# A graph layer and a two-expert FFN in one kernel: smaller layer-norm pieces, whole-pair selections, one engine for the last factor

## The chip, the cores and the metric

The kernel runs on one core of a Trainium2 chip. A core has five engines that run their own instruction streams and meet at semaphores: PE (TensorE, matrix products), DVE (VectorE, element-wise work and statistics), ACT (ScalarE, functions of the form f(scale·x + bias)), POOL (GpSimd, programmable; here it also writes the descriptors of gathers) and SP (SyncE, here only a queue that issues DMAs). Data lies in the on-chip memory of 128 partitions (SBUF); PE writes its sums into a second, small memory (PSUM).

The metric is the device time of one execution in microseconds (us), the median of several runs; less is better.

## The reference

Only what matters here:

```python
def _layernorm(x, axis=-1, eps=1e-05):
    return (x - mean(x)) / sqrt(var(x) + eps)

# x: 12500 nodes x 256; 200000 edges (src, dst, edge_weight), sorted by dst
def gnn(X, src, dst, val, W, b):
    msgs = (X @ W)[src] * val[:, None]
    return segment_sum(msgs, dst, 12500) + b

def ffn(x):                      # x[1, 12500, 256], 8 experts, hidden 512
    # routing from the mean over all nodes: the two best experts, weights tw
    out = sum over the two experts of tw_e * (gelu(x W1_e + b1_e) W2_e + b2_e)
    return layer_norm(out + x) * gamma + beta

x = x + gnn(_layernorm(x))
x = x + ffn(_layernorm(x)[None])[0]
```

## The kernel before, in words

Everything is float32. The work has three stages.

**First layer norm (lines 359 to 381).** `groups` cuts the 12500 nodes into pieces of up to R·128 nodes. With R = 8 there are 12 pieces of 1024 nodes (1 MB each) and two small ones, 14 in all. For each piece SP issues the load of `xt` (L362), DVE takes the statistics of each of the eight rows per partition (`row_stats`, L58 and L59), adds eps (L65), POOL raises to the power −1/2 (L66), DVE makes −mean/std (`nm`, L369), ACT writes the normalised rows in place (L373, eight instructions) and issues the store to `xn` in the chip's main memory (L376). ACT then clears one fourteenth of `acc`, the array of sums (L378). The pool `ln` has four buffers. `load_segment(0)`, three loads of edge data on SP (L297), stands ahead of the loop; `prepare_segment(0)` (L299 to L353: small DVE work, two products on PE, one copy on ACT) stands after the third piece.

**The gather loop.** Edges are taken 128 at a time as a column; four columns make a step and two steps a pair (`GB`, `SUPER`), so a pair has eight gathers. For each pair POOL issues eight indirect DMAs (`gather_pair`, L432), each of which brings 128 rows of `xn` by the 128 source indices of a column. `select` has DVE make, for each column, a 128x32 matrix with the edge's weight at its destination's place (`sel`, L415, with `iota`, `rel` and `wgt`) and for each step a 128x128 matrix `spread` (L423). `multiply` first has PE do a small product into `all_in` (L448) that reads every gathered column, so that later ones need no waits of their own, and then the eight products `pt` (L453); ACT copies them (L456), `spread_out` multiplies by `spread` (L468) and DVE adds into `acc` (L487). Between pairs the order written by hand in the main loop (with budgets in microseconds, `PAIR_US` and others) puts other work: `product`, `normalised` and `transposed` finish a block of 256 nodes whose sums are complete, and `work` runs parts of the experts' products (L604, L612) whose results go to `yts`.

**The end.** When the last pair is added, the last block is finished, the routing is computed, and 25 iterations follow, one for each group of up to 512 nodes, in a pipeline four deep. In an iteration `q` PE mixes the two experts' results (`mixed`), then `store(q-3)` has DVE add the node's own value (L849) and SP issue the output, `put(q-2)` multiplies by gamma (L843, on POOL when its number is odd and on DVE when it is even), `normalise(q-1)` has DVE make `nmt` (L833) and ACT normalise (L835), and `measured(q)` has DVE take statistics (L58, L59), add eps (L823) and POOL take the power (L825). Each engine works in this program order.

Of the kernel before, what the change touches and what calls it, by code (L numbers as in the profile page):

```python
# [18 lines left out]
P = 128  # L19
# [9 lines left out]
GB = 2  # L29
# [1 line left out]

NB = 8

R = 8

TB = 256
TPB = TB // P
# [24 lines left out]
def inv_std(nc, pool, out, var, half, rows, n):  # L62

    ve = pool.tile([P, R], FP, name="ve")
    nc.vector.tensor_scalar(ve[:rows, :n], var, EPS, None, ALU.add)  # L65
    nc.gpsimd.tensor_tensor(out, ve[:rows, :n], half[:rows, :n], ALU.pow)  # L66
# [30 lines left out]
def gnn_ffn_kernel(  # L97
# [43 lines left out]
    nc.vector.memset(ones, 1.0)  # L141
    row = const.tile([1, P], FP, name="row")
    nc.vector.memset(row, 1.0)
    zero = const.tile([P, 1], FP, name="zero")
    nc.vector.memset(zero, 0.0)
# [12 lines left out]
    viol = const.tile([P, 1], FP, name="viol")  # L158
    cand_f = const.tile([1, SLOTS], FP, name="cand_f")
    iota_i = const.tile([P, P], I32, name="iota_i")  # L160
    nc.gpsimd.iota(iota_i, pattern=[[1, P]], base=0, channel_multiplier=0)
    iota = const.tile([P, P], FP, name="iota")
    nc.vector.tensor_copy(iota, iota_i)
# [90 lines left out]
    with tc.tile_pool(name="rt", bufs=1) as rt, tc.tile_pool(  # L254
# [19 lines left out]
        def scratch_ps():  # L274
# [8 lines left out]
        nc.tensor.matmul(  # L283
            bias_ps.rearrange("p k d -> p (k d)"), row, bias_row.rearrange("p k d -> p (k d)"), start=True, stop=True
        )
        edgep = open_pool(name="edges", bufs=2)
        segment = {}

# [3 lines left out]
        def load_segment(k):  # L292
            s0, n = segs[k]
            t = {}
            for name, ap, dt in (("src_i", src, I32), ("dst_i", dst, I32), ("wgt", edge_weight, FP)):
                t[name] = edgep.tile([P, SEG * SUPER], dt, name=name)
                nc.sync.dma_start(t[name][:, : n * SUPER], ap[:, s0 * SUPER : (s0 + n) * SUPER])  # L297
            segment[k] = t
# [59 lines left out]
        cleared, part_n = 0, -(-(H * (NT * P + WIN)) // len(groups(N)))  # L358
        with tc.tile_pool(name="ln", bufs=4) as lp, tc.tile_pool(name="ln_s", bufs=8) as ls:
            for g, (r0, n, rows) in enumerate(groups(N)):  # L360
                xt = lp.tile([P, R, D], FP, name="xt")
                nc.sync.dma_start(xt[:rows, :n], x[r0 : r0 + rows * n].rearrange("(p r) d -> p r d", r=n))  # L362
                mv = ls.tile([P, R, 2], FP, name="mv")
                rs = ls.tile([P, R], FP, name="rs")
                nm = ls.tile([P, R], FP, name="nm")
                for r in range(n):
                    row_stats(nc, ls, mv[:rows, r], rows, xt[:rows, r])
                inv_std(nc, ls, rs[:rows, :n], mv[:rows, :n, 1], half, rows, n)
                nc.vector.scalar_tensor_tensor(  # L369
                    nm[:rows, :n], mv[:rows, :n, 0], -1.0, rs[:rows, :n], op0=ALU.mult, op1=ALU.mult  # L370
                )
                for r in range(n):
                    nc.scalar.activation(  # L373
                        xt[:rows, r], xt[:rows, r], AF.Identity, bias=nm[:rows, r : r + 1], scale=rs[:rows, r : r + 1]
                    )
                nc.scalar.dma_start(xn[r0 : r0 + rows * n].rearrange("(p r) d -> p r d", r=n), xt[:rows, :n])  # L376
                m = min(part_n, H * (NT * P + WIN) - cleared)
                nc.scalar.activation(acc_f[:, cleared : cleared + m], zero.to_broadcast([P, m]), AF.Copy)  # L378
# [12 lines left out]
        all_in = psum("in_ps", 1).tile([P, GB * SUPER], FP, name="all_in")  # L391

        w1 = expp.tile([P, SLOTS, H, F], FP, name="w1")
        w2 = expp.tile([P, SLOTS, FC, D], FP, name="w2")
# [10 lines left out]
        def select(i):  # L405

            s0, n = pairs[i]
            sel = selp.tile([P, GB * SUPER, NARROW], FP, name="sel")
            spread = selp.tile([P, GB, WIN], FP, name="spread")
            for j in range(n):  # L410
                k, at = seg_of(s0 + j)
                t = segment[k]
                for c in range(SUPER):
                    col = slice(at * SUPER + c, at * SUPER + c + 1)
                    nc.vector.tensor_scalar(  # L415
                        sel[:, j * SUPER + c],
                        iota[:, :NARROW],
                        t["rel"][:, col],
                        t["wgt"][:, col],
                        ALU.is_equal,  # L420
                        ALU.mult,
                    )
# [417 lines left out]
        def put(q, v):  # L840
            bb, n = mixes[q]
            m, t0 = n * TPB, bb * 2 * TPB
            (nc.gpsimd if q % 2 else nc.vector).tensor_tensor(  # L843
                v[:, :m], v[:, :m], gam.unsqueeze(1).to_broadcast([P, m, D]), ALU.mult
            )
            return v, m, t0
# [267 lines left out]
```

## Time and profile before

| what | value |
|---|---|
| median of three runs | 2258.58 us (2256.89 to 2259.1) |
| the profiled execution: its own time, its span | 2254.92 us, 2253.1 us |
| granted TensorE clock, mean | 0.865 |
| busy: PE, PE weight loads, DVE | 1506.6, 1175.2, 1173.3 us |
| busy: ACT, POOL | 523.3, 1573.4 us |
| first gather starts; last gather starts | 107.3 us; 2063.6 us |
| busy in 0 to 107.3 us: DVE, ACT, POOL | 58.99, 74.84, 22.10 us |
| busy in 2140.9 to 2253.1 us: PE, DVE, POOL | 71.13, 93.23, 54.33 us |

Span is the time from the first to the last instruction that the profiler saw. The page lists groups of instructions by line, engine, operation and tile, written output<-input; "x1564" is their count, then come busy microseconds and the mean nanoseconds of one, then the idle time of the engine just before them and what ended it. "issue" means that the engine waited for nothing that the profile shows.

### The profile page before, as it was taken

How to read it: one execution, taken by the hardware profiler on the slowest of the kernel's cores; microseconds unless marked ns; L12 is line 12 of the kernel's file. 1: busy time of each engine (PE TensorE's matmuls, PEld its weight loads, DVE VectorE, ACT ScalarE, POOL GpSimd, SP SyncE). 2: the span in 40 equal slices, each digit the busy share in tenths (PEclk: the TensorE clock that was granted, in tenths of full speed). 3: DMA queues.
4: the chain of work that ended last, by engine and by line, in shares of the span. 5: the costliest groups of instructions: out<-in, count | busy, mean ns of one | idle time of the engine just before them, and what ended most of it. 6: DMA issues, size and time to landing. Idle time of an engine off the chain costs nothing. (4 is left out here: it accounts for less than half of the span.)

```text
span 2253.1 us, 29981 instructions
## 1 busy us (share of the span) xinstructions
PE 1506.6 (67%) x9662; PEld 1175.2 (52%) x9662; DVE 1173.3 (52%) x4519; ACT 523.3 (23%) x1114; POOL 1573.4 (70%) x1626
## 2 busy tenths in 40 slices
PE   0034544445488888888765564988888888886875
PEld 0023333333267666666553343766666667664775
DVE  5535565655465565555454444544534443433687
ACT  5701111111122222222111111222222222221332
POOL 1277777777777777777777777777777777774254
PEclk9977677666799999999787776999999999999897
DMA  6634444444455555555544445555555545454585
GB/s 230 252 110 123 138 134 124 137 124 124 132 183 158 170 158 165 159 163 152 147 133 141 124 129 155 153 161 151 161 152 161 152 148 153 152 153 135 194 277 199
DMA packets 157377, 353.15 MB, mean 157 GB/s; under 512 B 34764, under 2 KB 65822, under 8 KB 154142
## 3 DMA queue, kind: packets, MB, share of 16 engines
q0 software_dynamic: 75072, 205.10, 32.0%
q1 hardware_dynamic: 79478, 132.85, 17.4%
q10 hardware_dynamic: 2664, 13.20, 1.4%
q8 instruction: 81, 1.33, 0.2%
q14 instruction: 82, 0.67, 0.1%
HBM read 286.89 MB, written 64.14 MB: 156 GB/s over the span
## 5 line engine op out<-in xcount | busy, mean ns | idle before, releaser
L432 POOL DMA_INDIRECT g<-xn,src_i x1564 | 1481.1, 947 | 485.0 <-issue 457.3
L487 DVE TENSOR_TENSOR acc<-acc,ps 128x256 f32 x391 | 164.0, 419 | 545.4 <-PE ps L468 397.5
L448 PE MATMUL all_in<-g,sel 128*32 128x8 f32 (+1 forms) x392 | 43.5, 185 | 591.9 <-issue 347.6
L604 PE MATMUL ph<-zTj,w 128*128 128x256 f32 x1568 | 388.8, 391 | 8.8 <-DMA zTj<-zts 8.8
L612 PE MATMUL po<-hT,w 128*128 128x256 f32 x1568 | 381.8, 388 | 12.3 <-DVE yT L618 12.3
L415 DVE TENSOR_SCALAR sel<-iota,rel,wgt 128x32 f32<-128x32 f32 x1564 | 371.6, 323 | 7.3 <-DMA xn<-xt 7.3
L448 PEld LDWEIGHTS all_in<-g,sel 128*32 128x32 f32 x392 | 29.9, 117 | 653.5 <-issue 551.0
L612 PEld LDWEIGHTS po<-hT,w 128*128 128x128 f32 x1568 | 303.1, 196 | 56.6 <-DVE yT L618 15.1
L604 PEld LDWEIGHTS ph<-zTj,w 128*128 128x128 f32 x1568 | 302.1, 198 | 50.1 <-issue 6.3
L456 ACT ACTIVATE part<-pt 128x512 f32<-128x512 f32 (+1 forms) x196 | 116.7, 595 | 844.4 <-PE pt L453 844.4
L468 PEld LDWEIGHTS ps<-spread,part 128*128 128x128 f32 x1564 | 250.2, 244 | 109.4 <-issue 109.4
L605 ACT ACTIVATE hT<-ph,b 128x256 f32<-128x256 f32 x392 | 185.6, 473 | 514.7 <-PE ph L604 514.7
L468 PE MATMUL ps<-spread,part 128*128 128x128 f32 x1564 | 293.6, 345 | 1.1 <-DVE acc L487 1.1
L453 PE MATMUL pt<-g,sel 128*32 128x256 f32 x3128 | 272.6, 470 | 0.0
L618 DVE SCALAR_TENSOR_TENSOR yT<-po,b,zTj 128x256 f32<-128x256 f32 x196 | 85.7, 479 | 252.2 <-PE po L612 251.0
L453 PEld LDWEIGHTS pt<-g,sel 128*32 128x32 f32 x3128 | 106.4, 127 | 43.5 <-issue 23.8
L512 PE MATMUL gz<-wg,acc 128*128 128x256 f32 x392 | 105.5, 416 | 24.9 <-ACT zT L545 13.9
L423 DVE TENSOR_SCALAR spread<-iota,slot 128x128 f32<-128x128 f32 x391 | 121.0, 309 | 0.0
L825 POOL TENSOR_TENSOR rst<-vet,half 128x4 f32<-128x4 f32 (+1 forms) x25 | 42.4, 1697 | 107.1 <-DVE vet L823 107.1
L512 PEld LDWEIGHTS gz<-wg,acc 128*128 128x128 f32 x392 | 78.7, 207 | 43.6 <-ACT zT L545 19.3
L513 DVE TENSOR_TENSOR acc<-gz,xt 128x512 f32<-128x512 f32 x49 | 33.9, 691 | 127.6 <-PE gz L512 127.6
L527 ACT ACTIVATE z<-acc,nmz,rstds 128x256 f32<-128x256 f32 x98 | 53.2, 591 | 128.1 <-DVE acc L487 117.0
(153 smaller groups left out, 1151.2 us busy)
## 6 DMA issues: line engine op xcount, KB each, us to landing
zTj<-zts SPq DMA_DIRECT2D x98, 256.0 KB
yts<-yT SPq DMA_DIRECT2D x98, 256.0 KB
g<-xn,src_i POOLq DMA_INDIRECT x1564, 2.8
ab<-yts SPq DMA_DIRECT2D x48, 512.0 KB
zts<-zT SPq DMA_DIRECT2D x49, 256.0 KB
xt<-in_x SPq DMA_DIRECT2D x12, 1024.0 KB
xn<-xt ACTq DMA_DIRECT2D x12, 1024.0 KB
xt<-in_x SPq DMA_DIRECT2D x48, 256.0 KB
```

Source lines behind the costliest of these rows:

```text
L415: nc.vector.tensor_scalar(sel[:, j * SUPER + c], iota[:, :NARROW], t["rel"][:, col], t["wgt"][:, col], ALU.is_equal, ALU.mult,)
L423: nc.vector.tensor_scalar(spread[:, j], iota[:, :WIN], t["slot"][:, at : at + 1], None, ALU.is_equal)
L432: nc.gpsimd.indirect_dma_start(out=g[:, j], out_offset=None, in_=xn, in_offset=bass.IndirectOffsetOnAxis(ap=segment[k]["src_i"][:, col : c ...
L453: nc.tensor.matmul(pt[q, j // SUPER], sel[:, j], g[:, j], start=True, stop=True, tile_position=(0, j % SUPER * NARROW))
L456: nc.scalar.activation(part[:, :n], pt[:, :n], AF.Copy)
L468: nc.tensor.matmul(ps[:, j, h], part[:, j, h * P : (h + 1) * P], spread[:, j], start=True, stop=True)
L487: nc.vector.tensor_tensor(at, at, ps[:, j], ALU.add)
L512: nc.tensor.matmul(ps[:, j], node_tile(t0 + j)[:, h], wg[:, h], start=(h == 0), stop=(h == H - 1))
L604: nc.tensor.matmul(ph, w1[:, k, h, c * P : (c + 1) * P], zT[:, h], start=(h == 0), stop=(h == H - 1))
L605: nc.scalar.activation(hT[:, c], ph, AF.Gelu, bias=b1[:, k, c : c + 1])
L612: nc.tensor.matmul(po[:, h], w2[:, k, c, h * P : (h + 1) * P], hT[:, c], start=(c == 0), stop=(c == FC - 1))
L618: nc.vector.scalar_tensor_tensor(yT[:, i], po[:, i], b2[:, k, i : i + 1], zT[:, i], op0=ALU.add, op1=ALU.add)
```

## The change

Eight edits:

1. `R` is 4: the first layer norm has pieces of 512 nodes (512 KB), 24 of them and two small ones, 26 in all, in nine buffers.
2. Its loop is split into `measure(g)` and `write(g)`; `write(g-1)` comes after `measure(g)`. `load_segment(0)` comes after `measure(1)`, `prepare_segment(0)` after the fifth piece.
3. A part of `acc` (128x975) is cleared by a POOL memset after each piece, not by ACT.
4. `iota_i` and `bias_row` lie in pools that are closed after use, and the two loads of `bias_row` stand beside the product that reads them.
5. `select` makes all eight `sel` matrices of a pair in two DVE instructions on 128x256 elements (compare, then multiply by the weight in place) and both `spread` matrices in one.
6. The small product that reads every gathered column goes to the head of `pt`; the PSUM tile `all_in` is gone.
7. `put` is always on POOL.
8. `zero` is gone, as nothing reads it.

```diff
-R = 8
+R = 4
...
-    bias_row = const.tile([1, 2, D], FP, name="bias_row")
-    nc.scalar.dma_start(bias_row[:, 0], b_gnn[None, :])
-    nc.scalar.dma_start(bias_row[:, 1], beta[None, :])
...
+        with tc.tile_pool(name="once", bufs=1) as once:
+            bias_row = once.tile([1, 2, D], FP, name="bias_row")
+            nc.scalar.dma_start(bias_row[:, 0], b_gnn[None, :])
+            nc.scalar.dma_start(bias_row[:, 1], beta[None, :])
+            nc.tensor.matmul(
+                bias_ps.rearrange("p k d -> p (k d)"), row, bias_row.rearrange("p k d -> p (k d)"), start=True, stop=True
+            )
...
-        load_segment(0)
-        with tc.tile_pool(name="ln", bufs=4) as lp, tc.tile_pool(name="ln_s", bufs=8) as ls:
-            for g, (r0, n, rows) in enumerate(groups(N)):
+        parts = groups(N)
+        with tc.tile_pool(name="ln", bufs=9) as lp, tc.tile_pool(name="ln_s", bufs=4) as ls:
+
+            def measure(g):
+                r0, n, rows = parts[g]
                 xt = lp.tile([P, R, D], FP, name="xt")
                 nc.sync.dma_start(xt[:rows, :n], x[r0 : r0 + rows * n].rearrange("(p r) d -> p r d", r=n))
...
+            measured_last = None
+            for g in range(len(parts)):
+                new = measure(g)
+                if g == 1:
+                    load_segment(0)
+                if measured_last:
+                    write(*measured_last)
+                measured_last = new
                 m = min(part_n, H * (NT * P + WIN) - cleared)
-                nc.scalar.activation(acc_f[:, cleared : cleared + m], zero.to_broadcast([P, m]), AF.Copy)
+                nc.gpsimd.memset(acc_f[:, cleared : cleared + m], 0.0)
                 cleared += m
-                if g == 2:
+                if g == 4:
                     prepare_segment(0)
+            write(*measured_last)
...
-            for j in range(n):
-                k, at = seg_of(s0 + j)
-                t = segment[k]
-                for c in range(SUPER):
-                    col = slice(at * SUPER + c, at * SUPER + c + 1)
-                    nc.vector.tensor_scalar(
-                        sel[:, j * SUPER + c], iota[:, :NARROW], t["rel"][:, col], t["wgt"][:, col],
-                        ALU.is_equal, ALU.mult,
-                    )
-                nc.vector.tensor_scalar(spread[:, j], iota[:, :WIN], t["slot"][:, at : at + 1], None, ALU.is_equal)
+            k, at = seg_of(s0)
+            t, m = segment[k], n * SUPER
+            cols = slice(at * SUPER, at * SUPER + m)
+            shape = [P, m, NARROW]
+            nc.vector.tensor_tensor(
+                sel[:, :m], iota[:, :NARROW].unsqueeze(1).to_broadcast(shape),
+                t["rel"][:, cols].unsqueeze(2).to_broadcast(shape), ALU.is_equal,
+            )
+            nc.vector.tensor_tensor(
+                sel[:, :m], sel[:, :m], t["wgt"][:, cols].unsqueeze(2).to_broadcast(shape), ALU.mult
+            )
+            shape = [P, n, WIN]
+            nc.vector.tensor_tensor(
+                spread[:, :n], iota[:, :WIN].unsqueeze(1).to_broadcast(shape),
+                t["slot"][:, at : at + n].unsqueeze(2).to_broadcast(shape), ALU.is_equal,
+            )
...
-                all_in[:NARROW, : n * SUPER], sel[:, n * SUPER - 1], g[:, : n * SUPER, 0], start=True, stop=True
+                pt[:NARROW, 0, : n * SUPER], sel[:, n * SUPER - 1], g[:, : n * SUPER, 0], start=True, stop=True
...
-            (nc.gpsimd if q % 2 else nc.vector).tensor_tensor(
+            nc.gpsimd.tensor_tensor(
                 v[:, :m], v[:, :m], gam.unsqueeze(1).to_broadcast([P, m, D]), ALU.mult
             )
```

More of the change, by code (lines that the diff above doesn't have):

```diff
@@ L143, in gnn_ffn_kernel @@
     nc.vector.memset(row, 1.0)
-    zero = const.tile([P, 1], FP, name="zero")
-    nc.vector.memset(zero, 0.0)
     wg = const.tile([P, H, D], FP, name="wg")
@@ L159, in gnn_ffn_kernel @@
     cand_f = const.tile([1, SLOTS], FP, name="cand_f")
-    iota_i = const.tile([P, P], I32, name="iota_i")
-    nc.gpsimd.iota(iota_i, pattern=[[1, P]], base=0, channel_multiplier=0)
     iota = const.tile([P, P], FP, name="iota")
-    nc.vector.tensor_copy(iota, iota_i)
+    with tc.tile_pool(name="once", bufs=1) as once:
+        iota_i = once.tile([P, P], I32, name="iota_i")
+        nc.gpsimd.iota(iota_i, pattern=[[1, P]], base=0, channel_multiplier=0)
+        nc.vector.tensor_copy(iota, iota_i)
     place_i = const.tile([P, 1], I32, name="place_i")
@@ L282, in gnn_ffn_kernel @@
         bias_ps = biasp.tile([P, 2, D], FP, name="bias_ps")
-        nc.tensor.matmul(
-            bias_ps.rearrange("p k d -> p (k d)"), row, bias_row.rearrange("p k d -> p (k d)"), start=True, stop=True
-        )
+        with tc.tile_pool(name="once", bufs=1) as once:
+            bias_row = once.tile([1, 2, D], FP, name="bias_row")
[4 more added lines that the diff above has]
+            )
         edgep = open_pool(name="edges", bufs=2)
@@ L353, in prepare_segment @@
             t.update(base_i=base_i, rel=rel, slot=slot)
-        load_segment(0)
         acc_f = acc.rearrange("p h n -> p (h n)")
-        cleared, part_n = 0, -(-(H * (NT * P + WIN)) // len(groups(N)))
-        with tc.tile_pool(name="ln", bufs=4) as lp, tc.tile_pool(name="ln_s", bufs=8) as ls:
-            for g, (r0, n, rows) in enumerate(groups(N)):
+        parts = groups(N)
+        cleared, part_n = 0, -(-(H * (NT * P + WIN)) // len(parts))
+        with tc.tile_pool(name="ln", bufs=9) as lp, tc.tile_pool(name="ln_s", bufs=4) as ls:
+            def measure(g):
+                r0, n, rows = parts[g]
                 xt = lp.tile([P, R, D], FP, name="xt")
@@ L364, in gnn_ffn_kernel @@
                 rs = ls.tile([P, R], FP, name="rs")
-                nm = ls.tile([P, R], FP, name="nm")
                 for r in range(n):
@@ L368, in gnn_ffn_kernel, with write @@
                 inv_std(nc, ls, rs[:rows, :n], mv[:rows, :n, 1], half, rows, n)
+                return g, xt, mv, rs
+            def write(g, xt, mv, rs):
+                r0, n, rows = parts[g]
+                nm = ls.tile([P, R], FP, name="nm")
                 nc.vector.scalar_tensor_tensor(
@@ L390, in gnn_ffn_kernel @@
         pps, aps = psum("part_ps", 1), psum("agg_ps", 1)
-        all_in = psum("in_ps", 1).tile([P, GB * SUPER], FP, name="all_in")
         w1 = expp.tile([P, SLOTS, H, F], FP, name="w1")
@@ L409, in select @@
             spread = selp.tile([P, GB, WIN], FP, name="spread")
-            for j in range(n):
-                k, at = seg_of(s0 + j)
-                t = segment[k]
-                for c in range(SUPER):
-                    col = slice(at * SUPER + c, at * SUPER + c + 1)
[L415 to L422, printed above, removed]
-                nc.vector.tensor_scalar(spread[:, j], iota[:, :WIN], t["slot"][:, at : at + 1], None, ALU.is_equal)
+            k, at = seg_of(s0)
[3 more added lines that the diff above has]
+            nc.vector.tensor_tensor(
+                sel[:, :m],
+                iota[:, :NARROW].unsqueeze(1).to_broadcast(shape),
+                t["rel"][:, cols].unsqueeze(2).to_broadcast(shape),
+                ALU.is_equal,
+            )
[4 more added lines that the diff above has]
+            nc.vector.tensor_tensor(
+                spread[:, :n],
+                iota[:, :WIN].unsqueeze(1).to_broadcast(shape),
+                t["slot"][:, at : at + n].unsqueeze(2).to_broadcast(shape),
+                ALU.is_equal,
+            )
             selections[i] = (sel, spread)
```

## The prediction

> **What bounds the kernel now.** I read the groups first, with the waits of the gathers; then the timeline at the two ends of the gather loop; then the few places in it where a gather was late.
>
> ```profile
> L432 POOL DMA_INDIRECT g<-xn,src_i x1564 | 1481.1, 947 | 485.0 <-issue 457.3
> ...
> L415 DVE TENSOR_SCALAR sel<-iota,rel,wgt 128x32 f32<-128x32 f32 x1564 | 371.6, 323 | 7.3 <-DMA xn<-xt 7.3
> ```
>
> The first gather starts at 107.30 us and the last at 2063.62, so 1563 periods take 1956.3 us, 1.252 us each: 0.946 in the instruction and 0.30 behind it for which the profile names no releaser ("issue"). POOL never waits for another engine there; its other waits in that stage come to some 19 us in slices of at most 0.3, the same gap under another name. So in the loop only what lengthens a gather counts, and no engine freed beside it pays. What comes before 107.3 and after 2063.6 counts fully. The timeline before it:
>
> ```profile
> 98.51 0.16 DVE L369 SCALAR_TENSOR_TENSOR nm<-mv,rs 84x1 f32<-84x1 f32 x1 [0.75 <-POOL rs L66]
> ...
> 104.69 0.34 ACTq L376 DMA_DIRECT2D xn<-xt  x1
> 105.07 1.70 ACT L378 ACTIVATE acc<-zero 128x1801 f32<-128x1801 f32 x1 [0.41 <-ACT xt L373]
> 107.30 1.21 POOL L432 DMA_INDIRECT g<-xn,src_i  x1 [8.82 <-ACT acc L378]
> ```
>
> Columns: start, duration, engine, line. DVE is done at 98.7, ACT at 106.8, with 14 clears of 1.71 us among its work; the last store of `xn`, issued at 104.69, lands about 106.4, and the gathers need it. In the loop, one place where a gather took 1.05 us and not 0.95:
>
> ```profile
> 958.44 0.29 DVE L344 SCALAR_TENSOR_TENSOR dst_f<-rel 128x128 f32<-128x128 f32 x1
> 958.50 1.05 POOL L432 DMA_INDIRECT g<-xn,src_i  x1 [0.30 <-issue]
> ```
>
> L344 reads two operands from SBUF. The same happens at 1438.07, to the hundredth. Last, two iterations of the end:
>
> ```profile
> 2197.90 0.17 DVE L823 TENSOR_SCALAR vet<-mv 128x4 f32<-128x4 f32 x1
> 2198.00 1.23 DVE L849 TENSOR_TENSOR ab<-ab,acc 128x1024 f32<-128x1024 f32 x1
> 2199.15 1.22 DVE L843 TENSOR_TENSOR ab<-ab,gam 128x1024 f32<-128x1024 f32 x1
> 2200.29 0.15 DVE L833 SCALAR_TENSOR_TENSOR nmt<-mv,rst 128x4 f32<-128x4 f32 x1
> ...
> 2202.63 0.17 DVE L823 TENSOR_SCALAR vet<-mv 128x4 f32<-128x4 f32 x1
> 2202.70 1.22 DVE L849 TENSOR_TENSOR ab<-ab,acc 128x1024 f32<-128x1024 f32 x1
> 2202.94 1.85 POOL L825 TENSOR_TENSOR rst<-vet,half 128x4 f32<-128x4 f32 x1 [2.85 <-DVE vet L823]
> 2204.76 2.34 POOL L843 TENSOR_TENSOR ab<-ab,gam 128x1024 f32<-128x1024 f32 x1
> 2204.82 2.30 DVE L833 SCALAR_TENSOR_TENSOR nmt<-mv,rst 128x4 f32<-128x4 f32 x1 [0.90 <-POOL rst L825]
> ```
>
> With gamma on DVE, `nmt` takes 0.15 us and the step from one L823 to the next is 4.73. With gamma on POOL, POOL goes straight from its power to L843, 0.06 us ahead of `nmt`, and `nmt` takes 2.30, as long as L843; the step is 6.68 (2202.63 to 2209.31). DVE is busy almost without a gap: it sets the end.
>
> **First layer norm: -26 us.** Removed from ACT: 14 x 1.71 = 24 us. What is left on ACT for a piece of four rows: 4 x 0.50 + 0.40 for the store's issue and some 0.1 = 2.5 us. DVE for such a piece: four statistics 2.27 us to L823's like (2138.62 to 2140.89 at the end, the same instructions), plus 0.18 for L65 and `nm` = 2.45. POOL: a power on 128x4 is 1.01 us where nothing disturbs it (L825 at 2102.07); the memset is not in the trace at this size, but 128x1 takes 0.10 and 128x128 0.205, 0.83 ns an element, so 128x975 is 0.91; together 1.92, hidden below 2.45. Without that cover (a memset over 1.4 us) each piece would be late by the rest. Since `nm` is made a piece later, DVE no longer stands still for POOL's power (1.75 us in each of 12 pieces).
> The start, with the queues: SP now issues two `xt` first, so the first lands at about 4.9 us, not 8.2 (1.4 us of issues less ahead of it, 1.4 us less for half the bytes, less traffic beside it). But the third thing on SP is `load_segment(0)`, whose memory was `bias_row`'s: it must wait for the bias product on PE, and that for `bias_row`'s two loads. Those land about 5.5 (the first did at 5.36), the product takes 2.04, so SP goes on at 7.9, issues three loads of edges (0.45 each) and at 9.3 the third `xt`, behind which all others queue. It lands about 12.4, and DVE, done with two pieces at 9.9, stands still 2.5 us. Then 22 pieces x 2.45 = 53.9. `prepare_segment(0)` took 10.0 us of DVE (27.64 to 37.64), 5.74 of them waiting for ACT's copy behind 4.04 + 1.71 us of other ACT work; now 2.0 + 0.4 stand ahead of it, a wait of about 2.2, so 6.5. DVE ends the last full piece at 12.4 + 53.9 + 6.5 = 72.8; ACT has that and two small pieces behind it, 0.8 + 4.0; 1.8 to land: 79.4. DMA must carry 2 x 512 KB in 2.45 us, 428 GB/s; the busy stretches of the old stage (66 to 79 us) moved 370 to 430. Nine buffers hold 4.6 MB of reads ahead, so it falls short by little: +2 us. First gather at 81.4 instead of 107.3. Bounds: 76 if DVE and ACT run freely, 90 if DMA moves 330 GB/s: a gain of 17 to 31.
>
> **Selections: +17.6 us.** DVE's burst of ten instructions (492.6 us in all, about 2.2 us a pair) becomes three on 128x256. The nearest row of that size is L487, 0.419 us, so 196 x 3 x 0.42 = 247. The 245 us saved lie beside POOL's gathers and are worth nothing. What counts is that each of the three reads two operands from SBUF, where the old ones read one. The late gather above started 0.06 us after L344 and lost 0.10, so L344 kept it off until 0.16 us after its own start. An element costs 1.04 ns (L487 with 256 takes 0.419 us, L550 with 512 takes 0.684), so that is 0.133 for its 128 plus 0.03; for 256 elements it is 0.296. A gather starts every 1.25 us, and bursts stand at all phases to it (I counted the old ones: no quarter of the period has under 13%). A gather loses on average half the lock when it starts inside it: 0.296 x 0.296 / 2 / 1.25 = 0.035 us per instruction, 0.105 per pair, x 196 = 20.6. The old excess of gathers over 0.946 goes, 3.0 us in all: +17.6.
> Here a page speaks otherwise. The Trainium skill, "SBUF — State Buffer", Who interferes with whom, says that VectorE's tensor_tensor takes only the read half of the ports shared with GpSimd, that descriptor generation needs the write half (marked as inferred), and that a probe saw no DMA stalled by it. By the page this part is -3.0, by the row +17.6. I take the row: this gather also reads its indices from SBUF, and the same section lets two SBUF inputs collide with a GpSimd instruction that reads. But it rests on two gathers. From below: -3. From above: if POOL loses also the race at the next of the back-to-back instructions, twice as much, +40.
> `all_in` moving into `pt`: PE must now wait for ACT's copy of the last `pt`, done some 2 us after a pair's products and 8 us before the next: 0; if that were late, the products behind would wait as before.
>
> **Gamma on POOL: +18.6 us.** From step 7 on (2140.89) steps are 6.68 and 4.73 in turn. Every even one becomes a 6.68: nine steps x 1.95 = 17.6, less 0.6 for one that waited for PE already (5.29). Of the earlier steps, which PE's experts' work holds at 6.2 to 6.9, one of 6.16 grows by 0.5. The last `put` is alone on the path: 2.34 - 1.22 = +1.1. The sum is 18.6. The 1.22 us that leave DVE in each even step are in this: the 2.30 of `nmt` replaces them. SP's output and load issues wait for L849 as before. Bounds 14 and 22.
>
> **Sum.** -26 + 17.6 + 18.6 = +10.2. The profiled execution took 2254.92 us (span 2253.1, so 1.8 around it) and would be 2265.1. It is 3.7 below the median of the runs, so I add the sum to the median: 2258.58 + 10.2 = 2268.8, and say 2269. Its own range, with gain 20 to 31, loop +10 to +27 and end +15 to +20 mostly not at their ends together: 2258 to 2279.
>
> **Rivals.** (1) Gathers do not feel the new selections (the page above). Place: each gather's start. Price: 20.6 us less. For it: two-element L80 and the PSUM-fed L487 and L508, 151 and 27 times at a gather's start, delay nothing, and only two gathers show L344's effect. Against: those read one SBUF operand or hold for nothing. Time 2258.6 - 26 - 3 + 18.6 = 2248, faster. It decides where the lock costs under 0.02 us per pair.
> (2) The start gains 12, not 26: SP's wait, or a queue of loads ahead of stores. For it: ACT's and SP's waits on shared DMA slots, and 82 us that SP waited for `xn` stores. Against: nine buffers. 2259 - 12 + 36 = 2283.
> (3) The loop loses 40: 2291. Against: between L849 and L843 on DVE, POOL's L825 got in at once (1.89 us, not 3).
> (4) `put` on POOL does not hold `nmt`: even steps 3.5, odd 4.4, 33 us less at the end, 2217. All ten odd steps shown speak against it.
>
> **How the numbers follow.** Forecast 0.62, (1) 0.14, (2) 0.14, (3) 0.08, (4) 0.02. The three runs lie within 0.1%, so 0.2% (4.5 us) is about what tells a change from none. Faster: (1), (4) and 0.03 of the forecast's range = 0.19. Same: 0.12 of it. Slower 0.69. The range of 8 in 10 takes (1) in and most of (2): 2247 to 2287.
>
> **What would show it.** First gather near 81 us (76 to 90), and SP standing at the first edge load until about 8. Mean start-to-start of gathers 1.262 to 1.264 us, with those that start within 0.3 us after a selection's start lasting up to 1.24; 1.250 would be rival (1). `nmt` near 2.3 us in all steps of the end and no step of 4.73. DVE busy near 930 us. It is wrong if the parts come out so and the sum does not: then a transfer at the loop's end or a lower clock in it is what I missed.

## The result, and the profile after

The changed kernel takes 2275.98 us (median of 4 runs, 2274.33 to 2276.31); the kernel before, run beside it on the same chip, takes 2257.73 (2254.53 to 2259.1). The ratio is 1.0081, interval 1.0064 to 1.0099: 0.8% slower, 18.2 us. The two profiled executions have spans of 2274.5 and 2253.1 us, 21.4 apart; the one of before was among its faster ones. By stages:

| us | before | after | difference | forecast |
|---|---|---|---|---|
| to the first gather | 107.30 | 89.11 | -18.2 | -26 |
| first to last gather | 1956.33 | 1971.01 | +14.7 | +17.6 |
| last gather to the end | 189.51 | 214.40 | +24.9 | +18.6 |
| span | 2253.1 | 2274.5 | +21.4 | +10.2 |

The groups of the changed kernel that answer to those of before:

```profile
L453 POOL DMA_INDIRECT g<-xn,src_i x1564 | 1495.9, 956 | 484.3 <-issue 463.0
...
L435 DVE TENSOR_TENSOR sel<-sel,wgt 128x256 f32<-128x256 f32 (+1 forms) x196 | 83.4, 425 | 6.7
L439 DVE TENSOR_TENSOR spread<-iota,slot 128x256 f32<-128x256 f32 (+1 forms) x196 | 82.2, 419 | 0.0
L429 DVE TENSOR_TENSOR sel<-iota,rel 128x256 f32<-128x256 f32 (+1 forms) x196 | 81.6, 416 | 0.0
```

The gathers are busy 14.8 us longer (1481.1 before), their idle time is 0.7 us shorter (485.0): all that the loop lost is inside the gathers. DVE, meanwhile, is busy 994.7 us in the execution instead of 1173.3, and nothing came of it. One place in the loop, in the timeline (start, duration, engine, line):

```profile
955.79 0.42 DVE L429 TENSOR_TENSOR sel<-iota,rel 128x256 f32<-128x256 f32 x1
955.87 1.16 POOL L453 DMA_INDIRECT g<-xn,src_i  x1 [0.30 <-issue]
```

The gather starts 0.08 us after the selection and takes 1.16 us, not 0.946. Over the whole trace 115 gathers start between 0.03 and 0.29 us after one of the three; 106 of them are late by more than 0.02 us, by 0.151 us on average, and nearly always by about 0.29 minus the offset (0.246 at 0.05, 0.19 at 0.10, 0.118 at 0.18, 0.014 at 0.28). The 115 lose 16.0 us in all. The ten gathers that start less than 0.03 us after a selection lose nothing.

The beginning, from several windows of the timeline:

```profile
9.20 0.33 SPq L297 DMA_DIRECT2D src_i<-in_src  x1
...
10.53 4.81 SPq L364 DMA_DIRECT2D xt<-in_x  x7
...
69.75 2.07 ACT L379 ACTIVATE xt<-xt,nm,rs 128x256 f32<-128x256 f32 x4 [0.46 <-DVE mv L59]
74.35 0.33 ACTq L382 DMA_DIRECT2D xn<-xt  x1
...
75.12 0.17 DVE L65 TENSOR_SCALAR ve<-mv 128x4 f32<-128x4 f32 x1
...
86.46 0.34 ACTq L382 DMA_DIRECT2D xn<-xt  x1
...
89.11 1.21 POOL L453 DMA_INDIRECT g<-xn,src_i  x1 [8.24 <-issue]
```

SP stood before its first edge load until 9.20 (the bias product ended at 9.17), so the third `xt` was issued only at 10.53. DVE was done with the last full piece at 75.3, but ACT issued its last store of `xn` at 86.46: ACT was 11 us behind, and 2.5 us of that is one store that ACT could have issued at 71.8 and issued at 74.35. The semaphores in the trace name the cause: the store uses the same one as the small `xt` load that SP had issued at 67.36, and goes out 0.07 us after that load's last signal (74.28). And two steps of the end:

```profile
2200.70 0.17 DVE L844 TENSOR_SCALAR vet<-mv 128x4 f32<-128x4 f32 x1
2200.81 1.22 DVE L870 TENSOR_TENSOR ab<-ab,acc 128x1024 f32<-128x1024 f32 x1
2201.01 1.88 POOL L846 TENSOR_TENSOR rst<-vet,half 128x4 f32<-128x4 f32 x1 [2.53 <-DVE vet L844]
2202.87 2.35 POOL L864 TENSOR_TENSOR ab<-ab,gam 128x1024 f32<-128x1024 f32 x1
2202.93 2.31 DVE L854 SCALAR_TENSOR_TENSOR nmt<-mv,rst 128x4 f32<-128x4 f32 x1 [0.90 <-POOL rst L846]
2207.43 0.17 DVE L844 TENSOR_SCALAR vet<-mv 128x4 f32<-128x4 f32 x1
```

From the seventh on, every step is now 6.7 us (here 2200.70 to 2207.43); the 4.73 of the even ones is gone, and `nmt` takes 2.3 us in each of these steps, as long as POOL's gamma beside it. (Of the first six `nmt`, three take 0.15 or 0.16.)

### The profile page after: what moved, and what is told of

The parts are those of the page before. It is cut to its first block, busy times and chain, and to the rows that moved or that the text cites. A ratio compares the mean times of both kernels' runs of the same rounds, so it can differ in the third digit from the quotient of the medians.

```text
span 2274.5 us, 28785 instructions
## 1 busy us (share of the span) xinstructions
PE 1537.7 (68%) x9662; PEld 1198.8 (53%) x9662; DVE 994.7 (44%) x3162; ACT 501.6 (22%) x1100; POOL 1644.1 (72%) x1677
## 4 chain that ended last, share of the span: by engine, by line
POOL 47%; issue 21%; PE 16%; DMA 8%; DVE 7%; ACT 1%; ACTq 0%; POOLq 0%; SPq 0%; DVEq 0%
POOL g L453 45%; DMA g<-xn,src_i 6%; PE ph L625 5%; PE po L633 4%; PE ps L489 3%; PE pt L474 2%; DVE st L58 2%; DVE nmt L854 2%; POOL rst L846 1%; PE gz L533 1%; DVE mv L59 1%; ACT xt L379 1%; DMA xt<-in_x 1%; DMA xn<-xt 0%; PE mix L829 0%
## 5 line engine op out<-in xcount | busy, mean ns | idle before, releaser
L469 PE MATMUL pt<-g,sel 128*32 128x8 f32 (+1 forms) x392 | 43.5, 185 | 581.2 <-DMA g<-xn,src_i 422.9
L469 PEld LDWEIGHTS pt<-g,sel 128*32 128x32 f32 x392 | 29.9, 117 | 643.3 <-issue 616.1
L489 PEld LDWEIGHTS ps<-spread,part 128*128 128x128 f32 x1564 | 259.3, 251 | 113.1 <-issue 112.6
L489 PE MATMUL ps<-spread,part 128*128 128x128 f32 x1564 | 303.7, 354 | 1.1 <-DVE acc L508 1.1
L474 PE MATMUL pt<-g,sel 128*32 128x256 f32 x3128 | 278.1, 478 | 0.0
L474 PEld LDWEIGHTS pt<-g,sel 128*32 128x32 f32 x3128 | 107.3, 127 | 44.7 <-issue 25.9
L533 PE MATMUL gz<-wg,acc 128*128 128x256 f32 x392 | 111.1, 433 | 24.3 <-ACT zT L566 13.9
L435 DVE TENSOR_TENSOR sel<-sel,wgt 128x256 f32<-128x256 f32 (+1 forms) x196 | 83.4, 425 | 6.7
L439 DVE TENSOR_TENSOR spread<-iota,slot 128x256 f32<-128x256 f32 (+1 forms) x196 | 82.2, 419 | 0.0
L429 DVE TENSOR_TENSOR sel<-iota,rel 128x256 f32<-128x256 f32 (+1 forms) x196 | 81.6, 416 | 0.0
```

The lines of the kernel that those rows point to most:

```text
L435: nc.vector.tensor_tensor(sel[:, :m], sel[:, :m], t["wgt"][:, cols].unsqueeze(2).to_broadcast(shape), ALU.mult)
L439: nc.vector.tensor_tensor(spread[:, :n], iota[:, :WIN].unsqueeze(1).to_broadcast(shape), t["slot"][:, at : at + n].unsqueeze(2).to_broadca ...
L474: nc.tensor.matmul(pt[q, j // SUPER], sel[:, j], g[:, j], start=True, stop=True, tile_position=(0, j % SUPER * NARROW))
L489: nc.tensor.matmul(ps[:, j, h], part[:, j, h * P : (h + 1) * P], spread[:, j], start=True, stop=True)
L533: nc.tensor.matmul(ps[:, j], node_tile(t0 + j)[:, h], wg[:, h], start=(h == 0), stop=(h == H - 1))
```

## The experiments

The table has every run; the stages are those of its profiled execution, the excess is what the gathers that took longer than the median gather (0.946 or 0.947 us) took over it, summed. Each ratio is to runs of the kernel before on the same chip, whose medians are 2256.92 to 2257.81 us.

| kernel | median us | ratio to before, interval | first gather | first to last | excess | last to end |
|---|---|---|---|---|---|---|
| before | 2257.73 | 1 | 107.30 | 1956.33 | 3.0 | 189.51 |
| after | 2275.98 | 1.0081 (1.0064-1.0099) | 89.11 | 1971.01 | 17.9 | 214.40 |
| before + selections | 2274.44 | 1.0073 (1.0056-1.0090) | 107.27 | 1972.09 | 19.1 | 192.99 |
| before + gamma on POOL | 2279.71 | 1.0095 (1.0078-1.0112) | 107.41 | 1956.78 | 3.6 | 215.72 |
| before + layer norm edits | 2236.19 | 0.9902 (0.9885-0.9918) | 87.61 | 1956.72 | 3.5 | 190.27 |
| after, selections by PSUM | 2257.66 | 0.9998 (0.9989-1.0006) | 88.28 | 1954.15 | 1.2 | 215.26 |
| after, gamma on DVE | 2238.17 | 0.9908 (0.9893-0.9923) | 86.76 | 1973.85 | 18.6 | 175.83 |
| after, shift made by POOL | 2241.98 | 0.9928 (0.9912-0.9943) | 87.15 | 1975.07 | 19.7 | 185.79 |
| after, last gamma on DVE | 2268.91 | 1.0047 (1.0033-1.0061) | 87.95 | 1973.59 | 18.2 | 208.09 |
| after, bias_row kept | 2271.26 | 1.0064 (1.0050-1.0078) | 83.04 | 1970.88 | 17.6 | 214.59 |
| before + clears on POOL | 2254.74 | 0.9992 (0.9985-0.9999) | 104.84 | 1955.86 | 2.7 | 190.45 |
| before + split loop | 2259.43 | 1.0010 (1.0003-1.0016) | 108.89 | 1957.14 | 4.0 | 190.56 |
| combination, old selections | 2215.51 | 0.9811 (0.9795-0.9828) | 83.92 | 1956.49 | 3.5 | 176.22 |
| combination, PSUM | 2211.95 | 0.9804 (0.9788-0.9821) | 83.61 | 1953.82 | 1.0 | 172.02 |

The theory after the result was: a gather that starts while DVE reads two operands from SBUF starts late; POOL's gamma holds DVE's `nmt`; and the start gave less because SP was held and ACT became the pace. The rival for the loop was that descriptors are written undisturbed and the loop grew for another reason, a lower clock (0.845 granted, 0.865 before) among them.

### One part at a time

The three-instruction selections in the kernel before:

```diff
-                    nc.vector.tensor_scalar(
-                        sel[:, j * SUPER + c],
-                        iota[:, :NARROW],
-                        t["rel"][:, col],
-                        t["wgt"][:, col],
...
-                nc.vector.tensor_scalar(spread[:, j], iota[:, :WIN], t["slot"][:, at : at + 1], None, ALU.is_equal)
+            nc.vector.tensor_tensor(
+                sel[:, :m],
+                iota[:, :NARROW].unsqueeze(1).to_broadcast(shape),
+                t["rel"][:, cols].unsqueeze(2).to_broadcast(shape),
...
+                sel[:, :m], sel[:, :m], t["wgt"][:, cols].unsqueeze(2).to_broadcast(shape), ALU.mult
...
+                spread[:, :n],
+                iota[:, :WIN].unsqueeze(1).to_broadcast(shape),
+                t["slot"][:, at : at + n].unsqueeze(2).to_broadcast(shape),
...
```

> The kernel before with the three-instruction selections alone; everything else, the extra PSUM tile all_in too, stays as before. Theory: a gather that starts while DVE is in an instruction with two SBUF operands begins late by up to 0.29 us. The loop from first to last gather should take 1971 us, as in the changed kernel (before 1956.3), the excess of gathers over 0.946 us should be near 18 us (before 3.0), and the time 2257.7 + 14.7 = 2272 us. Rival 1: descriptor writing is undisturbed, and the loop of the changed kernel grew for another reason (the reading product at the head of pt, the lower clock of 0.845): loop 1953 to 1957, time 2255 to 2258. Rival 2: the growth needs the other edits too (POOL's sequence, addresses in SBUF): in between.

Measured: 2274.44, loop 1972.09, excess 19.1. The gathers' group of this kernel:

```profile
L438 POOL DMA_INDIRECT g<-xn,src_i x1564 | 1497.0, 957 | 484.9 <-issue 457.8
```

The loss is there in full, with `all_in` in its old place and with a granted clock of 0.862. So neither the move of `all_in` nor the lower clock is the cause.

Gamma on POOL in the kernel before:

```diff
-            (nc.gpsimd if q % 2 else nc.vector).tensor_tensor(
+            nc.gpsimd.tensor_tensor(
```

> The kernel before with gamma on POOL in every step of the end. Theory: all steps from the ninth on take 6.7 us and nmt 2.3; from the last gather to the end 189.5 + 24.9 = 214 us, time 2257.7 + 25 = 2282 us, and the program ends with POOL's own closing work (6.6 us in the changed kernel) after its last multiplication. Rival: in the changed kernel the end also grew by the other edits (lower clock): then less than 20 us, 2276 or below.

Measured: 2279.71, end 215.72, clock 0.855. It grew as in the changed kernel; the steps from the seventh on are all 6.69 to 6.74 us.

The layer norm's edits alone (the changed kernel with the other two parts undone):

```diff
-            nc.vector.tensor_tensor(
-                sel[:, :m],
...
+                    nc.vector.tensor_scalar(
+                        sel[:, j * SUPER + c],
...
-                pt[:NARROW, 0, : n * SUPER], sel[:, n * SUPER - 1], g[:, : n * SUPER, 0], start=True, stop=True
+                all_in[:NARROW, : n * SUPER], sel[:, n * SUPER - 1], g[:, : n * SUPER, 0], start=True, stop=True
...
-            nc.gpsimd.tensor_tensor(
+            (nc.gpsimd if q % 2 else nc.vector).tensor_tensor(
```

> The changed kernel with the old ten-instruction selections, the old all_in tile and gamma alternating between POOL and DVE, so that only the edits of the first layer norm are left. Theory: first gather at 89 us, loop 1956 us, end 189.5 us; time 2257.7 - 18.2 = 2239.5 us. Rival: the early first gather is given back in the loop (its first gathers meet the last stores of xn, or the loop's start is not what bounds): 2248 to 2258 us, with the loop above 1960.

Measured: 2236.19, first gather 87.61, the loop unchanged. Nothing is given back. The three parts by their medians are +16.9, +22.1 and -21.4 against 2257.57: together +17.6, where the change measured +18.2. They add up within the scatter of the runs, so each can be judged alone.

### Why the gathers are late

The changed kernel with `iota` and the compare's result in PSUM, so that no selection instruction has two operands in SBUF:

```diff
+        both_ps = psum("sel_ps", 1).tile([P, P + GB * SUPER * NARROW], FP, name="both_ps")
+        iota_ps = both_ps[:, :P]
+        sel_ps = both_ps[:, P:].rearrange("p (c w) -> p c w", w=NARROW)
+        nc.vector.tensor_copy(iota_ps, iota)
...
-                sel[:, :m],
-                iota[:, :NARROW].unsqueeze(1).to_broadcast(shape),
+                sel_ps[:, :m],
+                iota_ps[:, :NARROW].unsqueeze(1).to_broadcast(shape),
...
-                sel[:, :m], sel[:, :m], t["wgt"][:, cols].unsqueeze(2).to_broadcast(shape), ALU.mult
+                sel[:, :m], sel_ps[:, :m], t["wgt"][:, cols].unsqueeze(2).to_broadcast(shape), ALU.mult
...
-                iota[:, :WIN].unsqueeze(1).to_broadcast(shape),
+                iota_ps[:, :WIN].unsqueeze(1).to_broadcast(shape),
```

> The changed kernel with iota and the result of the compare in PSUM, so that each of the three selection instructions has one operand in SBUF and one in PSUM; their number and sizes are the same. Theory: the delay comes from two operands in SBUF, as the PSUM-fed additions at L508 delay nothing: excess of gathers back to about 3 us, loop 1953 to 1957, time 2276 - 15 = 2261 us. Rival 1: any longer DVE instruction at a gather's start delays it, whatever it reads: loop 1971, time 2276. Rival 2: it is the lower clock or the reading product in pt: 2276 too, with no excess at the gathers' starts. Writing to PSUM may make the three instructions up to 0.1 us longer; nothing waits for them.

Measured: 2257.66, excess 1.2. Its groups, and one gather in its timeline:

```profile
L457 POOL DMA_INDIRECT g<-xn,src_i x1564 | 1479.0, 946 | 484.3 <-issue 470.9 <-DMA g<-xn,src_i 7.0 <-PE ph L629 3.0
L439 DVE TENSOR_TENSOR sel<-both_ps,wgt 128x256 f32<-128x256 f32 (+1 forms) x196 | 83.0, 424 | 6.7
L433 DVE TENSOR_TENSOR both_ps<-both_ps,rel 128x256 f32<-128x256 f32 (+1 forms) x196 | 82.9, 423 | 0.1
L443 DVE TENSOR_TENSOR spread<-both_ps,slot 128x256 f32<-128x256 f32 (+1 forms) x196 | 81.0, 413 | 0.0
```

```profile
1096.11 0.41 DVE L443 TENSOR_TENSOR spread<-both_ps,slot 128x256 f32<-128x256 f32 x1
1096.17 0.95 POOL L457 DMA_INDIRECT g<-xn,src_i  x1 [0.30 <-issue]
```

The instructions are as long as before (0.41 to 0.42 us) and as many, and 113 gathers start 0.03 to 0.29 us after one of them. None of these is late by more than 0.003 us, where 115 lost 16.0 us. L439 and L443 still write to SBUF, so it does not depend on where the result goes. Nor does it depend on DVE being in a long instruction when a gather starts; what counts is where that instruction's second operand lies.

### Why gamma on POOL costs

```diff
-            nc.gpsimd.tensor_tensor(
+            nc.vector.tensor_tensor(
```

> The changed kernel with gamma always on DVE, so that POOL has only the small power in each step of the end. Theory: nmt is held only by POOL's multiplication; without it every step from the eighth on takes 4.73 us, as the even ones before did, instead of 6.72: 17 x 1.99 = 34 us less, 4 us less after the last step (POOL's closing work is hidden again): time 2276 - 38 = 2238 us. Rival: some other engine (PE, the output's DMA) holds the steps at a value between, so that the gain is under 25 us: 2251 or more.

Measured: 2238.17, 37.8 us less. Two of DVE's own rows of this kernel:

```profile
2191.19 1.22 DVE L864 TENSOR_TENSOR ab<-ab,gam 128x1024 f32<-128x1024 f32 x1
2192.33 0.15 DVE L854 SCALAR_TENSOR_TENSOR nmt<-mv,rst 128x4 f32<-128x4 f32 x1
```

`nmt` is back at 0.15 us, and from the seventh on the steps are 4.69 to 4.97, but for two of 5.28 and 7.72. DVE's 1.22 us for gamma is cheaper than the 2.15 us by which `nmt` is longer when POOL does it.

Is it only `nmt` that stands, or whatever DVE does next? The shift in two parts, so that nothing on DVE needs POOL's power:

```diff
+            nc.vector.tensor_scalar(neg[:, :m], mv[:, :m, 0], -1.0, None, ALU.mult)
+            nc.gpsimd.tensor_tensor(nm[:, :m], neg[:, :m], rs[:, :m], ALU.mult)
...
-            nc.vector.scalar_tensor_tensor(nm[:, :m], mv[:, :m, 0], -1.0, rs[:, :m], op0=ALU.mult, op1=ALU.mult)
```

> The changed kernel with the shift (minus mean times the power) made in two: DVE negates the means, POOL multiplies by its own power straight after it, before gamma. Then no DVE instruction between POOL's power and POOL's gamma has to wait for the power. Theory: POOL's gamma costs because DVE's nmt, which needs POOL's power, comes just behind POOL's start of gamma and stands still as long as gamma runs; DVE's next two-operand instruction, the addition of the node's own value, comes 2.4 us later, after the statistics, so most of gamma runs beside them: steps of 4.4 to 5.2 us, 26 to 40 us less than 2276 (2236 to 2250). Rival: POOL is merely the slower engine or the hold falls on whatever DVE does next: steps near 6.7, time 2274 to 2280.

Measured: 2241.98, 34 us less, inside what the theory gave. But the profile (of an execution of 2249.8 us) shows it for a partly different reason:

```profile
2148.88 2.37 POOL L866 TENSOR_TENSOR ab<-ab,gam 128x1024 f32<-128x1024 f32 x1
2149.99 1.28 DVE L844 TENSOR_SCALAR vet<-mv 128x4 f32<-128x4 f32 x1
2151.19 0.16 DVE L848 TENSOR_SCALAR negt<-mv 128x4 f32<-128x4 f32 x1
```

The statistics, which read PSUM, ran freely beside gamma, as expected, but then `vet`, a small instruction with one operand, stood for 1.28 us until gamma ended at 2151.25; it takes 0.17 alone. I had expected the addition at L872 to be the first that could be held. The Trainium skill's "SBUF — State Buffer", Who interferes with whom, counts tensor_scalar among the instructions that can take the shared ports; this row agrees. So gamma on POOL can be half hidden (1.1 us of standing in such a step and not 2.15, and steps of 4.7), which makes it no better than gamma on DVE (3.8 us more by the medians). From the seventh step on, four are 8.1 to 9.6 us there; in one of them (2138.00 to 2146.42) DVE waited 2.5 us for PE, which had waited 3.1 us for the experts' results to be loaded. That load may be the next bound of a faster end; no run changes it.

### What comes after the last step

```diff
-            nc.gpsimd.tensor_tensor(
+            (nc.vector if q == len(mixes) - 1 else nc.gpsimd).tensor_tensor(
```

> The changed kernel with the very last multiplication by gamma on DVE, all others on POOL. Theory: of the 4.3 us that the end grew behind the last step, 1.1 is POOL's longer multiplication and the rest is POOL's closing work (a semaphore instruction of 1.8 us and a drain of 6.6), which before ran while DVE, SP and the output were still busy: from the last L844 to the end 15.7 us instead of 20.0, time 2272 us. Rival: the closing work comes last whatever POOL did before (it waits for the outputs): 19 us or more, time 2275 to 2276.

Measured: from the last L844 to the end 14.36 us, not 19.99, and 2268.91 us, 7 less. Part of those 7 lies elsewhere: the first gather came 1.2 us earlier in its profile, the loop was 2.6 longer, and the end 6.3 shorter. In the trace POOL closes the program with a semaphore instruction of 1.78 us and a drain of 6.60 us, the same in all kernels. In the kernel before the drain ended at 2250.44, and POOL waited 1.9 us for the others; in the changed kernel it starts at 2267.08, ends at 2273.68, and everything else waits for it. Here it ends at 2268.33 and the others 0.5 later.

### The beginning

```diff
-        with tc.tile_pool(name="once", bufs=1) as once:
-            bias_row = once.tile([1, 2, D], FP, name="bias_row")
-            nc.scalar.dma_start(bias_row[:, 0], b_gnn[None, :])
-            nc.scalar.dma_start(bias_row[:, 1], beta[None, :])
...
+    bias_row = const.tile([1, 2, D], FP, name="bias_row")
+    nc.scalar.dma_start(bias_row[:, 0], b_gnn[None, :])
+    nc.scalar.dma_start(bias_row[:, 1], beta[None, :])
```

> The changed kernel with bias_row back among the constants and its two loads issued with them, so that the edge loads on SP do not stand behind the bias product. Theory: the third xt is issued 3 to 4 us earlier than 10.53, DVE no longer stands still from 9.8 to 15.0, and the first gather comes 3 to 5 us earlier, at 84 to 86 instead of 89.1: time 2271 to 2273 us. Rival: ACT's queue, which falls behind DVE by 0.12 us a piece and stands 2.5 us for a DMA slot near the end, sets the first gather whatever the beginning is: 88 to 90, time 2275 to 2277.

Measured: 2271.26, first gather 83.04. Its timeline:

```profile
6.83 3.46 SPq L363 DMA_DIRECT2D xt<-in_x  x7
...
10.43 0.43 DVE L58 BATCH_NORM_STATS2 st<-xt 128x6 f32<-128x256 f32 x1 [1.00 <-DMA xt<-in_x]
...
83.04 1.21 POOL L452 DMA_INDIRECT g<-xn,src_i  x1 [8.24 <-issue]
```

The third `xt` is issued 3.7 us earlier, its statistics start at 10.43 instead of 15.02, and 4.7 us come out in the time. ACT's pace does not swallow it, because ACT starts earlier too. SP's wait was a price of the edit that put `bias_row` into memory that is used again.

What of the gain is the clears' and what the split loop's? First the clears alone, in the kernel before:

```diff
-                nc.scalar.activation(acc_f[:, cleared : cleared + m], zero.to_broadcast([P, m]), AF.Copy)
+                nc.gpsimd.memset(acc_f[:, cleared : cleared + m], 0.0)
```

> The kernel before with the array of sums cleared by a POOL memset (128x1811, 14 of them) and not by ACT; the pieces stay at 1024 nodes in four buffers, the loop is not split. The forecast took the 24 us of clears off ACT as the main part of the gain at the start. Theory: by the trace of before, the 6.37 us of a piece are as much DVE's (its statistics and then 1.75 us of standing for POOL's power) as ACT's, so the clears alone give only ACT's lag at the end: first gather 101 to 103 instead of 107.3, time 2257.5 - 5 = 2252 us; the rest of the 18 us comes from the split loop and the smaller pieces. Rival: the clears are all of it: first gather near 89, time 2240.

Measured: 2254.74, 0.1% less; first gather 104.84, a smaller gain than the 101 to 103 expected. Two pieces in its timeline:

```profile
42.29 0.17 DVE L369 SCALAR_TENSOR_TENSOR nm<-mv,rs 128x8 f32<-128x8 f32 x1 [1.75 <-POOL rs L66]
...
48.66 0.17 DVE L369 SCALAR_TENSOR_TENSOR nm<-mv,rs 128x8 f32<-128x8 f32 x1 [1.75 <-POOL rs L66]
48.86 4.04 ACT L373 ACTIVATE xt<-xt,nm,rs 128x256 f32<-128x256 f32 x8 [2.33 <-DVE nm L369]
```

A piece still takes 6.37 us (42.29 to 48.66): ACT is free earlier and waits 2.33 us for DVE, which stands 1.75 for POOL's power. Then the split alone:

```diff
-            for g, (r0, n, rows) in enumerate(groups(N)):
+            def measure(g):
...
+            def write(g, xt, mv, rs):
...
+            for g in range(len(parts)):
+                new = measure(g)
+                if measured_last:
+                    write(*measured_last)
+                measured_last = new
...
+            write(*measured_last)
```

> The kernel before with the loop of the first layer norm split into measure(g) and write(g-1), and nothing else: pieces of 1024 nodes in four buffers, the clears on ACT, the edge loads ahead, the preparation after the third piece. Theory: ACT's 6.37 us for a piece (4.04 + 0.33 + 1.71 and gaps) and DVE's 6.37 (statistics and the 1.75 of standing for POOL's power) are two bounds of equal height; the clears taken away alone brought 2.5 us at the first gather, and the standing taken away alone should bring no more: first gather 104 to 110 (the first normalisation comes a piece's statistics later), time 2255 to 2260. Rival: DVE alone was the bound, and the split alone brings most of it: first gather below 95, time under 2246.

Measured: 2259.43, 0.1% more; first gather 108.89. Its ACT rows:

```profile
48.47 1.71 ACT L392 ACTIVATE acc<-zero 128x1811 f32<-128x1811 f32 x1 [0.40 <-ACT xt L380]
50.08 4.02 ACT L380 ACTIVATE xt<-xt,nm,rs 128x256 f32<-128x256 f32 x8
...
54.52 1.71 ACT L392 ACTIVATE acc<-zero 128x1811 f32<-128x1811 f32 x1 [0.41 <-ACT xt L380]
```

Here ACT does not wait (later it does twice, 2.8 and 1.6 us, for DVE), and a piece is 6.05 us of ACT. The clears alone bring the first gather 2.5 us nearer and the split alone puts it 1.6 us off; together, with the smaller pieces in nine buffers and the two queues' new order, they give 18 to 20. What the size and the number of buffers give by themselves was not tried.

### A better kernel

Layer norm edits, `bias_row` kept, gamma on DVE in every step; with the old selections, or with the three by PSUM:

```diff
-            nc.gpsimd.tensor_tensor(
+            nc.vector.tensor_tensor(
...
+    bias_row = const.tile([1, 2, D], FP, name="bias_row")
```

> The changed kernel's first layer norm with bias_row kept among the constants, the old ten-instruction selections and gamma always on DVE. By the single results: 2257.5 - 21.4 (layer norm) - 4.7 (bias_row) - 16 (steps of 4.7 in place of 6.68 and 4.73 in turn: eight odd steps by 1.95) = 2215 us, if each part is independent of the others. If they overlap, 2220 to 2236.

> As the other combination, but with the three-instruction selections, iota and the compare in PSUM. The old selections cost gathers some 3 us of delay, the PSUM form 1.2: the loop should take 1954 us instead of 1956.7 and the whole 2 to 3 us less than the other combination, near 2213 us. If the ten smaller instructions disturb as little as three, the two are equal to within 1 us.

Measured: 2215.51 and 2211.95, as the single results add up. Both are faster than the kernel before and the changed one: ratios of 0.981 and 0.980 to before. The intervals of the two overlap, so the advantage of the PSUM form over the old selections is only suggested by the medians; its loop is 2.7 us shorter, and its excess is 1.0 us instead of 3.5.

## Why the prediction was right, and where it was off

The prediction was 2269 us, slower by 10; it was slower by 18. The direction was right, and so was the main mechanism of each of the three parts. Two terms of the sum were mis-sized, both to the bad side; by luck the third came out 2.9 us better than forecast and covered part of that.

**"Selections: +17.6 us".** Right: the loop grew by 14.7 in the pair of profiles, and the selections alone cost 16.9 by the medians. The lock of 0.296 us read from two late gathers is 0.29 over 106 of them. The two small errors: 115 gathers began inside it rather than the 139 that an even spread over phases gave (ten more began in the first 0.03 us, which holds nobody; the rest is that bursts are not quite even against the gathers), so that they lost 16.0 us and not 20.6; and of the old excess of 3.0 us, taken as gone, 1.8 stayed. The loop's mean period is 1.261 us, a little under the 1.262 to 1.264 named. Rival (1), the rule of the Trainium skill that a tensor_tensor disturbs no descriptor writing ("SBUF — State Buffer", Who interferes with whom, which marks its reason as inferred), does not hold for these gathers. By that section a second SBUF operand collides with a POOL instruction that reads, which is what the PSUM form bears out; which read of the gather it is, its indices or something else, was not tried.

**"First layer norm: -26 us".** This term failed by 7.7 us in the profile: -18.2, and -21.4 in the time. Steps of it, in order. "SP goes on at 7.9": it went on at 9.20, because the bias product began at 7.13 and not 5.5 (it waited for the second of its two loads), and the data of the third piece could be used at 15.02, not 12.4; 2.6 us. I saw this wait and priced it too low, and its whole cost is 4.7 us of time, as the kernel with `bias_row` kept shows. "22 pieces x 2.45": DVE took 2.41, so that step was right, and it ended at 75.3 for the forecast 72.8. "ACT has that and two small pieces behind it, 0.8 + 4.0": failed. I had ACT's work for a piece as 2.5 us and DVE's as 2.45 and let DVE set the pace. ACT's rows are 2.53 apart, so ACT falls behind by 0.12 a piece, about 2.4 us over twenty, and one store stands 2.5 us for the semaphore that it shares with a load (1.2 to 2.5 us in the other kernels with the same loop). ACT ended at 86.43, 11.1 us behind DVE and not 4.8; the last 1.4 of these 6.3 us I have not divided. Against that, 2.7 us passed from there to the first gather, and not 3.8. That the clears were the gain's source, as "Removed from ACT: 24 us" suggests, is only part of it: without the end of DVE's standing, which the prediction names too, they bring 2.5 us.

**"Gamma on POOL: +18.6 us".** The main step was right: the steps from the seventh on gave 17.8 us (the even ones 17.4) for the forecast 17.0, with `nmt` at 2.3 us in each, and the earlier ones 0.6 for 0.5. "The last `put` is alone on the path: +1.1" failed: from the last L844 to the end it is +4.3. POOL's last 8.4 us of closing work had always been there, hidden behind DVE and the output; giving POOL the last multiplication pushed it out to the end. The rest of the 24.9 in the profile, 2.3 us from the last gather to the first L844, is not gamma's: that stretch is 34.3 us in the profile of before, 36.5 in the changed kernel and 34.4 to 37.9 in the others, whether gamma is on POOL or not. By the medians gamma costs 22.1.

**The other signs.** No step of 4.73 was left, as said. DVE is busy 994.7 us and not 930: the old instructions overlap one another, so that DVE was busy with them for 430 us and not the 492.6 that the two groups give together, and 245 us was more than DVE's real saving; no step rested on it. Rival (2), a start worth 12, and rival (3), a loop worse by 40, did not come; (4) was refuted by every step from the seventh on.

## What to carry to other kernels

When an engine writes descriptors or runs small work beside DVE, look first at where DVE's operands lie: three long instructions with two SBUF operands cost gathers more than ten short ones with one, though they halve DVE's time for the selections (430 us to 231), and the same three with one operand in PSUM cost nothing. Handing a DVE multiplication to POOL is a loss where DVE's next instruction needs the same ports: count what DVE stands still (2.15 us), not what it is spared (1.22). Where two engines have nearly the same pace, cost the edits together: alone, one brought 2.5 us and the other nothing, and both with smaller pieces 18 to 20; and see what an edit's reused memory makes a load queue wait for.

## What the runs showed of the hardware that I had not expected

- POOL's closing work is 1.78 us and then 6.60 us in every kernel here; with a last instruction of POOL on the path it is exposed, some 3 us in this one.
- A tensor_scalar on 128x4 with one operand is held by POOL's tensor_tensor (1.28 us instead of 0.17), while statistics reading PSUM pass beside it. The same operation in the old selections, on 128x32 and 128x128, hardly delayed a gather (2.1 us over the 365 that started up to 0.5 us behind one).
- In the changed kernel a gather had to be 0.03 us or more behind the start of the DVE instruction to be held; the ten that were nearer took their 0.946 us. The hold ends 0.29 us after that start, before the instruction does (0.42 us).
- A store on ACT's queue stood 2.5 us for a load on SP's queue that used the same semaphore.
